# The first router's second pass goes on beside the end of its first pass, and its one-hots are multiplied on VectorE

## The chip, the cores and the metric

One core of a Trainium2 chip runs the whole program in one launch. The metric is the time of one execution in microseconds (us), on the device. Engines are named as in the profile: PE (TensorE: matrix products; PEld is its loading of weights), DVE (VectorE), ACT (ScalarE), POOL (GpSimd) and SP (the queue that issues most DMAs). Each engine works through its own instructions in order.

## The reference

The input x is 8 sequences of 512 tokens with 256 features, float32. Three sublayers follow one another, each on the layer-normalised x and added to x: half of a mixture-of-experts feed-forward, a sparse attention (each token attends to its 8 most similar earlier ones), and again half of the same feed-forward. The feed-forward is

```python
probs = softmax(xf @ gate_w.T); weights, idx = top_k(probs, 2)
weights = weights / weights.sum(-1)
out_all[e] = (silu(xf @ w1[e].T) * (xf @ w3[e].T)) @ w2[e].T      # 8 experts, 512 hidden
result = sum over the token's 2 experts of weight * out_all[expert]
```

Only the two chosen experts of each token need to be computed.

## The kernel before, in words

**Tiles.** The 4096 tokens make 8192 (token, expert) pairs in each feed-forward. A router sorts them by expert into tiles of 256 slots (`SLOTS`), in two halves of 128 rows. A tile does `fetch_weights` (one DMA of 1.5 MB from SP, its row read out of `wrow`), `fetch_rows` (two indirect gathers on POOL, L649, by the `tokens` table), `turn` (four transposes `ptx` on PE, L688, and their copy `xT` on DVE, L690), four times `up` (eight PE instructions `ph`, L699; `silu` on ACT, L707; the product `g` on DVE, L708), twice `down` (`py` on PE, L714) and twice `put` (scaling on ACT, L725, and an indirect DMA on POOL that adds the rows to `out`, L726). Weights and rows are fetched three tiles ahead.

**The first router's two passes.** `route` is a generator that goes on by one small step at each `next`. It runs twice for the first feed-forward: for sequences 0 to 3 (`select` is `begin`, kind "full") and 4 to 7 (`others`, kind "rest", `share=True`); both have `times=True`. The first pass gives the tables of the first four tiles (0 to 3 below), the second those of the following ones (rest 0, rest 1, ...). A pass counts the pairs, works out each pair's slot (`dest` L448 to L451; `at` and its reductions, L457 and L319; `slot`, `lane`, `group`, `cell`, `value`, L460 to L469), and then, in eight turns r = 0, 4, ..., 28 of four columns, builds one-hots: `in_lane` (L504) and `in_group` (L509) on DVE, and `put`, which is `in_group` times `value` (L518) and times `wts`. In the first pass both products run on POOL (L518, L526). In the second the first runs on POOL and the second as four activations on ACT (L524). PE multiplies `put` and `in_lane` into `pl` (L494, eight instructions a turn). Along with it goes `select.choose` (`free`, `pk` L572, `rank` to `owners` L575 to L603, `pw` L606, `wrow` L612). At the end come the addition to the table (L539), its transposes `pT` on PE (L621), their copy `tableT` (L624), the products `po` (L629), and `tokens` and `wslot` (L642, L645); the gathers wait for `tokens`.

**The order.** All of this part stands under a schedule written by hand: each engine's queue is in the order of the program. A list of steps runs both passes side by side (`half(0)`, `half(1)`) between statistics and normalisations. A loop (L1057 to L1060) then takes the first pass to its end. After it, what is left of the second pass is in `routing`, and `side`, called some six times a tile between the tile's PE work, takes it on by one step each time (`route_on`). `side` also takes on the normalisation of sequences 4 to 7 on ACT (`opening`, L979) and later the attention.

```python
        while halves[0].gi_frame is not None:
            if begin.wrow is not None and tiles[0].w is None:
                tiles[0].fetch_weights()
            half(0)
        derive_parameters()
    routing = [halves[1]]
```

`derive_parameters` (L146 to L157) issues three ACT functions (Sigmoid, Exp, Ln), each with a load of its function table, and some small DVE operations.

Of the kernel before, what the change touches and what calls it, by code (L numbers as in the profile page):

```python
# [28 lines left out]
def kernel(  # L29
# [14 lines left out]
    nc = tc.nc  # L44
# [91 lines left out]
    def load_parameters():  # L136
        for n in range(P // DH):
            nc.sync.dma_start(wkq_sb[:, :, n, :], (wqT if n % 2 else wkT).rearrange("(k p) h -> p k h", p=P))
        nc.sync.dma_start(gain_sb, gain.to_broadcast([P, D]))
        nc.sync.dma_start(bias_sb, bias.to_broadcast([P, D]))  # L140
        nc.sync.dma_start(mix_in, log_mix.to_broadcast([P, 1]))
        nc.sync.dma_start(scale_in, log_scale.to_broadcast([P, 1]))

    def derive_parameters():

        nc.scalar.activation(mix, mix_in, AF.Sigmoid)  # L146
        nc.vector.tensor_scalar(rest, mix, -1.0, 1.0, ALU.mult, ALU.add)
        nc.vector.tensor_scalar(mix_gain, gain_sb, mix, None, ALU.mult)

        sp_abs = const.tile([P, 1], F32, tag="sp_abs", name="sp_abs")  # L150
        nc.vector.scalar_tensor_tensor(sp_abs, scale_in, -1.0, scale_in, ALU.mult, ALU.min)
        sp_exp = const.tile([P, 1], F32, tag="sp_exp", name="sp_exp")
        nc.scalar.activation(sp_exp, sp_abs, AF.Exp)
        sp_log = const.tile([P, 1], F32, tag="sp_log", name="sp_log")
        nc.scalar.activation(sp_log, sp_exp, AF.Ln, bias=1.0)
        nc.vector.scalar_tensor_tensor(scale, scale_in, 0.0, sp_log, ALU.max, ALU.add)
        nc.vector.tensor_scalar(scale, scale, 0.01, None, ALU.add)  # L157
# [106 lines left out]
    def clear_rows():  # L264
        for t in (rows_d, out):
            nc.sync.dma_start(
                t[:PAD, :].rearrange("(h p) d -> p h d", p=P), zeros.unsqueeze(1).to_broadcast([P, PAD // P, D])
            )
# [24 lines left out]
    def route(ffn, s0, S, select, times=False, share=False):  # L293
# [195 lines left out]
        def chunks(t, r):  # L489
            return t.rearrange("p i j -> p (i j)")[:, r : r + R].unsqueeze(2)  # L490

        def multiply(r, in_lane, put):
            for q in range(R):
                nc.tensor.matmul(  # L494
                    pl, lhsT=in_lane[:, q, :], rhs=put[:, q, :, :ng], start=(r + q == 0), stop=(r + q == 2 * J - 1)
                )
# [3 lines left out]
        for r in range(0, 2 * J, R):  # L500
            if len(built) > 1:
                multiply(*built.pop(0))
            in_lane = small.tile([P, R, P], F32, tag="in_lane", name=f"in_lane_{name}_{r}", bufs=3)
            nc.vector.tensor_tensor(  # L504
                in_lane, lane_of.unsqueeze(1).to_broadcast([P, R, P]), chunks(lane, r).to_broadcast([P, R, P]),
                ALU.is_equal,
            )
            in_group = small.tile([P, R, NG], F32, tag="in_group", name=f"in_group_{name}_{r}", bufs=2)
            nc.vector.tensor_tensor(  # L509
                in_group[:, :, :ng], group_of[:, :ng].unsqueeze(1).to_broadcast([P, R, ng]),  # L510
                chunks(group, r).to_broadcast([P, R, ng]), ALU.is_equal,
            )
            if not times:
                yield
                if built:
                    multiply(*built.pop(0))
            put = small.tile([P, R, 2, NG], F32, tag="put", name=f"put_{name}_{r}", bufs=3)
            (nc.gpsimd if times else nc.vector).tensor_mul(  # L518
                put[:, :, 0, :ng], in_group[:, :, :ng], chunks(value, r).to_broadcast([P, R, ng])
            )  # L520
            if share:
                for q in range(R):
                    w = wts.rearrange("p i j -> p (i j)")[:, r + q : r + q + 1]
                    nc.scalar.activation(put[:, q, 1, :ng], in_group[:, q, :ng], AF.Copy, scale=w)  # L524
            else:
                (nc.gpsimd if times else nc.vector).tensor_mul(put[:, :, 1, :ng], in_group[:, :, :ng], chunks(wts, r).to_broadcast([P, R, ng]))  # L526
            built.append((r, in_lane, put))
            next(choice, None)
            yield
# [405 lines left out]
    def load(b):  # L935
        tag, bufs = ("xin", 4) if b < HALF_B else ("x1", 3) if b < B - 1 else ("own", 2)
        xb = work.tile([P, NC, D], F32, tag=tag, name=f"xin_{b}", bufs=bufs)
        nc.sync.dma_start(xb, x[b].rearrange("(c p) d -> p c d", p=P))
        xin.append(xb)
# [19 lines left out]
    def keep_rows(b):  # L959
        nc.sync.dma_start(seq_rows(out, first_ffn, b), xin[b])  # L960
# [24 lines left out]
    def gates(b):  # L985
        first_ffn.gates(b, columns[b])

    halves = [
        route(first_ffn, 0, HALF_B, begin, times=True),
        route(first_ffn, HALF_B, HALF_B, others, times=True, share=True),  # L990
    ]

    def half(i):
        next(halves[i], None)
# [43 lines left out]
    with tc.manual_schedule():  # L1038
        def load_columns(b):
            nc.sync.dma_start(columns[b].rearrange("p k t -> p (k t)"), xT[b].rearrange("p k t -> p (k t)"))  # L1040

        for b in range(HALF_B):
            load_columns(b)
            if b:
                load(b - 1)
        load(HALF_B - 1)
        clear_rows()
        for b in range(HALF_B, B):
            load_columns(b)
            load(b)  # L1050
        load_parameters()
        for step in steps:
            for f, b in step:
                f(b)
        for b in range(HALF_B):
            keep_rows(b)
        while halves[0].gi_frame is not None:  # L1057
            if begin.wrow is not None and tiles[0].w is None:
                tiles[0].fetch_weights()
            half(0)  # L1060
        derive_parameters()
    routing = [halves[1]]

# [19 lines left out]
    def finish_on():  # L1083

        nonlocal ended
        if finishing:
            b, steps = finishing[0]
            next(steps, None)
            if steps.gi_frame is None:
                finishing.pop(0)  # L1090
                ended = b + 1
                if ended in routes:
                    routing.append(route(*routes[ended]))
# [177 lines left out]
```

## Time and profile before

| what | value |
|---|---|
| median of 3 runs | 1052.44 us (1049.25 to 1053.2) |
| the profiled execution, its own time | 1052.27 us |
| its span, first to last instruction | 1050.5 us |
| mean granted TensorE clock | 0.985 |
| first `up` of tile 0 starts | 77.41 us |
| `up` of tiles 1, 2, 3, rest 0, rest 1 starts | 92.83, 115.81, 128.25, 141.24, 152.04 us |

The page gives the busy time of each engine, then groups of instructions by line with the idle time ahead of them; "PE pl_f L494 <- POOL put_f L518" is PE's wait at line 494 for what POOL wrote at line 518. In the timeline a row holds start, duration (from the first start to the last end of merged ones), engine, line, operation, output and inputs, and in brackets the engine's idle time ahead of it and what ended it. A table by stretch of time gives each engine's busy time in it, then the granted clock, the DMA engines' share and GB/s.

### The profile page before, as it was taken

Reading aid. Unit: us, or ns where it says so; the run is one execution under the profiler, and the core shown is the slowest. Engines: PE = TensorE matmul, PEld = TensorE weight load, DVE = VectorE, ACT = ScalarE, POOL = GpSimd, SP = SyncE. Lnnn points to the kernel's source line nnn. Section 1 sums busy time; section 2 is a strip of 40 time slices with the busy share of each in tenths; the row PEclk is TensorE's granted clock in tenths of the full one; section 3 lists DMA queues with packets and bytes.
Section 4 is the critical chain, followed back from the end, with each engine's and each line's share of the span. In section 5 each row is a group of like instructions: output and inputs, shape, how many; then the busy total and the mean of one; then the engine's idle time right before and its main releaser. Section 6 shows DMA issues by size and latency. Waiting matters only on the chain. (4 is left out here: it accounts for less than half of the span.)

```text
span 1050.5 us, 14816 instructions
## 1 busy us (share of the span) xinstructions
PE 985.9 (94%) x5008; PEld 853.0 (81%) x5008; DVE 545.5 (52%) x1838; ACT 383.7 (37%) x814; POOL 442.3 (42%) x434
## 2 busy tenths in 40 slices
PE   6768999999999999999999999999999999999984
PEld 6657888888787878878788787887888888889973
DVE  5954212124566665978649787587844422222221
ACT  1726222222645364363443633536313122212211
POOL 1133254546353354624425325253335454546343
PEclk9999999999999999999999999999999999999987
DMA  9557366666454546535436455363556565767665
GB/s 341 170 208 243 96 206 185 197 203 181 149 148 153 178 135 194 177 112 161 120 113 189 138 161 153 110 190 110 162 170 183 182 199 171 217 181 209 204 215 159
DMA packets 66164, 183.14 MB, mean 174 GB/s; under 512 B 8288, under 2 KB 51040, under 8 KB 56736
## 3 DMA queue, kind: packets, MB, share of 16 engines
q1 hardware_dynamic: 39216, 145.11, 39.9%
q0 software_dynamic: 26592, 36.98, 17.1%
q8 instruction: 44, 0.72, 0.3%
q14 instruction: 40, 0.33, 0.1%
q10 hardware_dynamic: 272, 0.01, 0.0%
HBM read 146.94 MB, written 35.13 MB: 173 GB/s over the span
## 5 line engine op out<-in xcount | busy, mean ns | idle before, releaser
L699 PE MATMUL ph_f_s<-xT_f_s,w_f_s 128*128 128x256 f32 (+1 forms) x2368 | 500.1, 365 | 4.2 <-ACTq L1218 3.4
L699 PEld LDWEIGHTS ph_f_s<-xT_f_s,w_f_s 128*128 128x128 f32 x2368 | 423.3, 193 | 71.4 <-issue 11.3
L726 POOL DMA_INDIRECT out<-y_f_s,tokens_f_s x133 | 215.8, 1622 | 399.5 <-ACT y_f_s L725 363.4
L708 DVE TENSOR_TENSOR g_f_s<-silu_f_s,ph_f_s 128x256 f32<-128x256 f32 (+1 forms) x296 | 117.1, 397 | 404.9 <-ACT silu_f_s L707 404.7
L714 PE MATMUL py_f_s<-w_f_s,g_f_s 128*128 128x256 f32 x1088 | 254.7, 384 | 0.0
L714 PEld LDWEIGHTS py_f_s<-w_f_s,g_f_s 128*128 128x128 f32 x1088 | 202.3, 192 | 25.3 <-issue 0.5
L707 ACT ACTIVATE silu_f_s<-ph_f_s 128x256 f32<-128x256 f32 (+1 forms) x296 | 108.4, 367 | 309.6 <-PE ph_f_s L699 303.4
L649 POOL DMA_INDIRECT xr_f_s<-rows_d,tokens_f_s x146 | 146.1, 1001 | 50.8 <-issue 32.3
L725 ACT ACTIVATE y_f_s<-py_f_s,wslot_f_s 128x256 f32<-128x256 f32 x133 | 56.3, 471 | 197.3 <-PE py_f_s L714 195.5
L707 ACT ACT_TABLE_LOAD x41 | 52.6, 1283 | 8.0 <-PE ph_f_s L699 7.4
L688 PE MATMUL ptx_f_s<-ident,xr_f_s 128*128 128x128 f32 x288 | 45.0, 277 | 10.4 <-DMA xr_f_s<-rows_d,tokens_f_s 10.4
L690 DVE COPY xT_f_s<-ptx_f_s 128x512 f32<-128x512 f32 x72 | 49.2, 683 | 9.4 <-PE ptx_f_s L688 9.4
L494 PE MATMUL pl_f<-put_f,in_lane_f 128*128 128x156 f32 (+4 forms) x256 | 43.9, 325 | 7.8 <-POOL put_f L518 4.0
L688 PEld LDWEIGHTS ptx_f_s<-ident,xr_f_s 128*128 128x128 f32 x288 | 36.0, 142 | 18.2 <-DMA xr_f_s<-rows_d,tokens_f_s 8.0
L494 PEld LDWEIGHTS pl_f<-put_f,in_lane_f 128*128 128x128 f32 x256 | 41.2, 230 | 10.2 <-POOL put_f L526 4.9
L750 POOL TENSOR_TENSOR own<-xn_at,mix_gain 128x1024 f32<-128x1024 f32 x8 | 19.5, 2434 | 59.7 <-DVE a_f L199 32.3
L1161 POOL MEMSET apart<- 128x1 f32 x62 | 44.0, 709 | 0.0
L825 ACT ACT_TABLE_LOAD x31 | 39.8, 1283 | 2.4 <-DVE nmax L814 1.9
L518 POOL TENSOR_TENSOR put_f<-in_group_f,value_f 128x184 f32<-128x184 f32 (+1 forms) x16 | 9.9, 621 | 72.1 <-DVE free_f_s L565 41.4
L783 PE MATMUL psim<-xnT_at 128*128 128x128 f32 (+3 forms) x128 | 40.0, 435 | 0.0
L844 PE MATMUL pm<-xn_at,exT 128*128 128x256 f32 x160 | 39.9, 380 | 0.0
L844 PEld LDWEIGHTS pm<-xn_at,exT 128*128 128x128 f32 x160 | 29.8, 190 | 3.7
(250 smaller groups left out, 901.0 us busy)
## 6 DMA issues: line engine op xcount, KB each, us to landing
w_f_s<-in_wexp SPq DMA_DIRECT2D x73, 1536.0 KB, 6.9
rows_d<-xn_f SPq DMA_DIRECT2D x16, 512.0 KB, 3.2
columns<-in_xT SPq DMA_DIRECT2D x8, 512.0 KB, 8.3
xin<-in_x SPq DMA_DIRECT2D x8, 512.0 KB, 9.2
out<-xin SPq DMA_DIRECT2D x8, 512.0 KB, 5.4
x<-out SPq DMA_DIRECT2D x8, 512.0 KB, 3.9
out<-x SPq DMA_DIRECT2D x8, 512.0 KB, 5.0
xr_f_s<-rows_d,tokens_f_s POOLq DMA_INDIRECT x146, 3.8
```

What stands on the lines that cost most here:

```text
L494: nc.tensor.matmul(pl, lhsT=in_lane[:, q, :], rhs=put[:, q, :, :ng], start=(r + q == 0), stop=(r + q == 2 * J - 1))
L649: nc.gpsimd.indirect_dma_start(out=dst, out_offset=None, in_=table, in_offset=bass.IndirectOffsetOnAxis(ap=index.bitcast(U32), axis=0),)
L688: nc.tensor.transpose(pt[:, k, h * P : (h + 1) * P], xr[:, k * P : (k + 1) * P], ident)
L690: nc.vector.tensor_copy(self.xT, pt)
L699: nc.tensor.matmul(ph[:, n, slots], lhsT=wn[:, k, f * P : (f + 1) * P], rhs=self.xT[:, k, slots], start=(k == 0), stop=(k == KD - 1),)
L707: nc.scalar.activation(s[:, slots], ph[:, 0, slots], AF.Silu)
L708: nc.vector.tensor_mul(self.g[:, f, slots], s[:, slots], ph[:, 1, slots])
L714: nc.tensor.matmul(self.py[:, h, :], lhsT=self.g[:, f, h * P : (h + 1) * P], rhs=self.w2[:, f, :], start=(f == 0), stop=(f == KF - 1),)
L725: nc.scalar.activation(y, self.py[:, h, :], AF.Copy, scale=self.routed.wslot[:, c])
L726: add = nc.gpsimd.indirect_dma_start(out=self.acc_d, out_offset=bass.IndirectOffsetOnAxis(ap=self.routed.tokens[:, c].bitcast(U32), axis=0 ...
L844: nc.tensor.matmul(pm[:, :D], lhsT=exTs[c][:, s * P : (s + 1) * P], rhs=after if c == 0 and s == 1 else xn[:, s, :], start=(s == 0), stop= ...
L1161: nc.gpsimd.memset(apart, 0.0)
```

## The change

The loop at the end of the opening takes the second pass on by one step with each step of the first, and in the second pass (`share`) DVE does the first product instead of POOL. The second product stays on ACT.

```diff
             put = small.tile([P, R, 2, NG], F32, tag="put", name=f"put_{name}_{r}", bufs=3)
-            (nc.gpsimd if times else nc.vector).tensor_mul(
+            (nc.gpsimd if times and not share else nc.vector).tensor_mul(
                 put[:, :, 0, :ng], in_group[:, :, :ng], chunks(value, r).to_broadcast([P, R, ng])
             )
...
             if begin.wrow is not None and tiles[0].w is None:
                 tiles[0].fetch_weights()
             half(0)
+            half(1)
         derive_parameters()
```

In each engine's queue this moves the following. DVE: `at`, `slot` to `value`, and the turns 0, 4 and 8 with their puts, `free`, `rank` to `owners` now stand ahead of the first pass's `tokens`; turn 12 stands ahead of tile 0's `xT`; turns 16 to 24 stand in tile 0, turn 28 behind tile 1's `xT`. PE: `pk`, `pl` of turns 0 and 4 and `pw` stand ahead of tile 0, the other six `pl` groups within tile 0, the second pass's `pT` and `po` in tile 1 (before: in tile 2). ACT: `put` of turns 0 to 12 ahead of the table loads of `derive_parameters`, the Ln load behind tile 0's first `silu`, and one more Silu load behind that. POOL: the eight products are gone, and rest 0's gathers stand ahead of tile 2's accumulates (before: behind them). SP: the order is the same.

## The prediction

> **What bounds the kernel now.** The page's busy shares come first, because they say whose time can be saved; then the waits of PE from 77 to 152 us, the stretch that the diff touches; then the timeline around the two waits, and the granted clock by stretch.
>
> ```profile
> PE 985.9 (94%) x5008; PEld 853.0 (81%) x5008; DVE 545.5 (52%) x1838; ACT 383.7 (37%) x814; POOL 442.3 (42%) x434
> ```
> PE is busy 94% of the span. From about 150 us on it hardly waits, so what moves its work there by some us moves the end as much. The gaps lie ahead of that.
>
> ```profile
> PE pl_f L494 <- POOL put_f L518: 4.0, 1, 4.0
> PE ptx_f_s L688 <- DMA xr_f_s<-rows_d,tokens_f_s: 1.8, 1, 1.8
> ```
> Between 77 and 152 us PE waits twice at length: once for a GpSimd one-hot product of the second pass, once for a gather. The timeline shows why:
>
> ```profile
> 71.10 0.17 DVE L642 TENSOR_TENSOR tokens_f_s<-po_f_s,cell_of 128x8 int32<-128x8 f32 x1 [1.96 <-PE po_f_s L629]
> 77.41 8.77 PE L699 MATMUL ph_f_s<-xT_f_s,w_f_s 128*128 128x256 f32 x32 [0.78 <-DVE xT_f_s L690]
> ...
> 99.45 1.38 POOL L649 DMA_INDIRECT xr_f_s<-rows_d,tokens_f_s  x1 [0.30 <-issue]
> 100.86 1.37 POOL L518 TENSOR_TENSOR put_f<-in_group_f,value_f 128x312 f32<-128x312 f32 x2
> 101.63 2.45 PE L494 MATMUL pl_f<-put_f,in_lane_f 128*128 128x156 f32 x8 [4.04 <-POOL put_f L518]
> ```
> VectorE had that put's one-hot by 93.2 us, but GpSimd's queue held two accumulates (94.29, 96.24) and two gathers (98.12, 99.45) ahead of it. The last column is the wait: 4.04 us of an idle PE. Then the clock:
>
> ```profile
> 86.00:92.80 6.80, 6.80 (x43) 6.08 (x41) 5.35 (x15) 5.22 (x17) 2.39 (x3) 1.00 0.78 263
> 92.80:101.60 8.80, 4.79 (x27) 4.03 (x25) 2.95 (x7) 6.56 (x19) 6.49 (x7) 0.97 1.03 323
> 101.60:106.00 4.40, 4.37 (x17) 4.10 (x18) 0.97 (x1) 1.11 (x4) 1.34 (x2) 0.66 0.93 311
> 141.20:152.00 10.80, 10.80 (x53) 9.51 (x53) 2.28 (x5) 2.38 (x6) 5.33 (x5) 1.00 0.66 195
> ```
> The column before the last two is the granted clock: 0.66 behind the gap. The last row is a tile undisturbed: 10.80 us, all of it PE.
>
> **Unit prices, from the timeline, start to start.** Four 256-column products of `up` (eight instructions): 1.73 us (silu at 82.76 and 84.49). One `pl` group of eight: 1.06 (88.84 to 89.90). VectorE: in_lane 0.60, in_group 0.40 (89.76, 90.36, 90.76). The new VectorE put, 312 elements, stands in the trace in the second router: 0.48 us, so a dependent in_group and put take 0.52 + 0.40, and a triple 1.52.
>
> **Price 1: the first tile starts later.** The listing of the changed build's order puts this on VectorE, in one queue, between `dest` (its last operation at 66.27) and the first tokens:
> - the two `at` products and reductions, 1.39 (81.79 to 83.18): the table add (L539) goes from 67.07 to 67.95;
> - slot to value 0.70 (83.52 to 84.24), triple 0 (1.52) and two `free` operations (0.15): tableT starts at 67.95 + 0.22 + 0.70 + 1.52 + 0.15 = 70.54, not 68.46; PE's transposes would be ready at 69.35, so VectorE sets it;
> - tableT 0.60, triples 4 and 8 (3.04), rank to owners (0.79): tokens at 74.97 instead of 71.10.
>
> That is **3.87 us later**. PE's own order is no later: `pk` ends at 71.7, `po` (1.87) at 73.6, two `pl` groups at the slow rate (2.24 each, from 101.63 to 103.87) at 78.1, `pw` at 78.7, and the first gathered rows land at 74.56 + 3.87 = 78.43, the second at 79.6. GpSimd has nothing ahead of the gathers, ACT's put parts (1.11 each) end before their `pl`. xT_0 waits behind triple 12 on VectorE, which ends at 77.7, before 80.54. So `up` starts at 77.41 + 3.87 = 81.28. Bounds: three puts at GpSimd's mean of 0.747 add 3 x 0.27 = 0.8; at VectorE's 152-element row, 0.31, they take off 0.5. I take the row of the same engine and size.
>
> **What is saved, from tile 0 to the second rest tile.** Before, `up` of tiles 0, 1, 2, 3, rest 0, rest 1 starts at 77.41, 92.83, 115.81, 128.25, 141.24, 152.04: 74.63 us. Its ledger: five tiles at 10.80 = 54.0; eight `pl` groups 8.48; `pk` and `pw` 0.61; `pT` and `po` 1.64 (12.44 - 10.80); first `up` group slow 1.72 (3.45 instead of 1.73); the wait 4.04; slow products behind it 1.5 (2.24 and 2.08, instead of 1.06 and 1.73); rest 0's late gather 2.19 (12.99 - 10.80). Sum 74.2; 0.4 is unassigned and stays.
>
> After:
> - The wait and its slow products go: **-5.54**. The puts no longer queue on GpSimd.
> - Two `pl` groups, `pk` and `pw` run in the gap ahead of tile 0, where PE waits for rows: **-2.73**.
> - Rest 0's gather goes from behind tile 2's accumulates to ahead of them, because the pass's tokens, at 124.80 before, come with tile 1's end at about 110: **-2.19**. Its other conditions are met: the last normalised rows are written at about 109 us, the gather issues at about 118, and its rows are wanted at about 131. SP's order is the same, and its weight fetches still wait for PE, tile by tile.
> - New: ACT in tile 0. Its queue now holds five table loads instead of four (1.28 us each); two of them fall inside tile 0. From silu_0 at 84.91: itself 0.40, Ln load and sp_log 1.52, two normalisations 0.98, put 16 1.04, Silu load 1.30, so silu_1 at 90.15; then two normalisations, a put that waits for its in_group and a silu in turn give silu_3 at 96.05 and g_3 at 96.87. PE, at 1.73 and 1.06 a group, wants g_3 at 95.92: **+1.0**. PE then reaches tile 1 at about 101.2. Bounds: 0 if ACT keeps pace; +1.4 more if put's four activations cost their busy mean (4 x 0.347 = 1.39, not 1.03).
> - The diff's VectorE work inside tiles 0 and 1 hides under ACT's waits (VectorE idles half of that stretch).
>
> Sum: -5.54 - 2.73 - 2.19 + 1.0 + 3.87 = **-5.6 us**. The profiled execution took 1052.27 (span 1050.5 and 1.77 around it, taken as constant); 1052.27 - 5.6 = **1046.7**. It lies 0.17 below the median of the runs shown, 1052.44, so no correction is made.
>
> **The clock of tile 0.** The first eight `up` products took 3.45 us at 77.41, the next 1.73: PE starts slow (the clock column reads 1.00 there, so the durations are the evidence). I keep that price, since 92-column `pl` groups stayed slow (2.02 for eight at 53.2, after 7 us of nearly unbroken work). But in the changed kernel 4.5 us of 156-column groups end at 78.1, and behind the gap at 101.63 just such a group and part of an `up` brought full speed after 2.8 us. [...]
>
> **Rivals.**
> - *PE is fast when tile 0 begins.* The 156-column groups release the clock, and the 3.2 us from 78.1 to 81.28, with transposes only, don't take it back. Then 1.72 goes: 1046.7 - 1.7 = 1045.0. For it: the speed-up at 104.4. Against: the 3.2 us, nearly the time after which the gap at 97.6 cost the clock. Chance 0.22.
> - *ACT becomes the bound of tile 0, or the gather stays late.* With ACT's longer activations (+1.4) and a GpSimd-priced put (+0.8) 1048.9; with rest 0's wait kept instead (+2.2) the same. For it: ACT's queue from 84.9 to 99.7 is full. Against: no such ACT pitch in the trace. Chance 0.22.
> - *Slower: tile 0 runs at half clock.* Its `up` groups come one at a time between `pl` groups that wait for ACT, so PE may never work densely enough. Tile 0 with its six groups is 17.2 us at full speed; each us of it at half clock costs one more. Beyond the 1.72 priced, 5.6 us of it pass the break-even; all of it gives 1046.7 + 15.4 = 1062. Against: the clock stayed 1.00 from 81 to 92.8 with the same alternation. Chance 0.04.
> - *That nothing moves* is excluded by the order listing.
>
> The forecast has 0.52. Half a per cent (5.3 us, to 1047.2) is about what a measurement of this kernel can tell from no change. The forecast lies beside that bound: some 0.31 of its 0.52 falls below, with 0.20 of the first rival and 0.02 of the second: faster 0.53. Nearly all else is same, 0.42, and the last rival with a little for what I haven't seen is slower, 0.05. The range takes in the first rival and most of the second: 1044.0 to 1049.5.
>
> **What would show it.** Tokens of the first pass at about 75 us and `up` at 81.3; no PE wait on a GpSimd put; first `up` group 3.45 us (or 1.7: first rival); g_3 and `pl` in tile 0 waiting for ACT about 1 us in all; tile 1 at 101, tile 2 at 113.6, rest 1 at 146.4; no wait for rows ahead of rest 0. It is wrong if tile 0 starts after 83, if tile 0 takes over 21 us, or if the lead at rest 1 is lost later.

## The result, and the profile after

The changed kernel takes 1045.07 us (median of 11 runs, 1040.95 to 1048.92), the kernel before beside it 1051.84 us (11 runs, 1049.25 to 1053.2). The ratio is 0.9937, with a 95% interval of 0.992 to 0.9955: faster by 0.6%, 6.8 us. The forecast was 1046.7, with 1044.0 to 1049.5 as its range.

The busy times hardly move (PE 985.9 us before, 984.2 after): what went is waits. The first fence is the page's line of busy times after the change, the second holds PE's waits between 77 and 152 us (in all, times, longest):

```profile
PE 984.2 (94%) x5008; PEld 852.3 (82%) x5008; DVE 547.5 (52%) x1846; ACT 384.9 (37%) x815; POOL 435.1 (42%) x426
```
```profile
PE ptx_f_s L688 <- DMA xr_f_s<-rows_d,tokens_f_s: 1.3, 2, 0.9
PE ph_f_s L699 <- issue: 0.8, 1, 0.8
PE py_f_s L714 <- DVE g_f_s L708: 0.7, 1, 0.7
```

The wait for a POOL product at L518, 4.0 us before, is gone from the second list. New in it is `py` waiting for `g`, 0.7 us. The timeline of PE shows where tile 0 now stands:

```profile
78.40 0.33 PE L688 MATMUL ptx_f_s<-ident,xr_f_s 128*128 128x128 f32 x1 [0.38 <-DMA xr_f_s<-rows_d,tokens_f_s]
79.66 0.55 PE L688 MATMUL ptx_f_s<-ident,xr_f_s 128*128 128x128 f32 x3 [0.93 <-DMA xr_f_s<-rows_d,tokens_f_s]
80.99 3.68 PE L699 MATMUL ph_f_s<-xT_f_s,w_f_s 128*128 128x256 f32 x8 [0.79 <-issue]
84.50 1.23 PE L494 MATMUL pl_f<-put_f,in_lane_f 128*128 128x156 f32 x8
85.56 1.89 PE L699 MATMUL ph_f_s<-xT_f_s,w_f_s 128*128 128x256 f32 x8
...
96.51 0.70 PE L714 MATMUL py_f_s<-w_f_s,g_f_s 128*128 128x256 f32 x2 [0.69 <-DVE g_f_s L708]
```

Read three things in it. Tile 0's first `up` is at 80.99 (77.41 before). It takes 3.5 us until `pl` starts at 84.50, the next one 1.73 (85.56 to 87.29): half speed, then full speed. The 0.69 in brackets at 96.51 is the wait for `g_3`. The table by stretches has PE's busy time behind the length of the stretch, and the granted clock in the column before the last two. The stretches here are those between the changes that this trace records of the clock:

```profile
74.22:77.63 3.41, 3.41 (x15) 1.00 0.09 25
77.63:81.04 3.41, 1.31 (x9) 1.00 0.30 93
81.04:84.45 3.41, 3.41 (x8) 0.50 0.38 115
```

The first change on record is at 77.63, and ahead of it the column reads 1.00 although the durations are those of half speed: the last `pl` products in the gap take 0.26 us each up to there, and 0.13 at full speed. So PE came to full speed at 77.63, fell to half at 81.04, just as tile 0 began, and was back at full speed at 84.45.

The starts of `up`, from the timelines, tell where each kernel of this study gains. From the first rest tile on all run at 10.80 us a tile, so the last column but one, 152.04 less the start of rest 1, is the lead that a kernel carries into the rest of its run. Each ratio is to runs of the kernel before beside it; the medians come from several sessions:

| kernel | tile 0 | tile 1 | rest 1 | lead at rest 1 | median, and ratio to before with its interval |
|---|---|---|---|---|---|
| before | 77.41 | 92.83 | 152.04 | 0 | |
| changed | 80.99 | 100.89 | 145.73 | 6.31 | 1045.07, 0.9937 (0.992 to 0.9955) |
| changed, second time | 81.12 | 101.14 | 145.98 | 6.06 | 1043.96, 0.9914 (0.9888 to 0.9939) |
| e1: product on DVE alone | 77.38 | 94.35 | 147.68 | 4.36 | 1045.27, 0.9951 (0.9935 to 0.9967) |
| e2: extra step alone | 80.97 | 100.99 | 145.82 | 6.22 | 1043.35, 0.993 (0.991 to 0.9949) |
| e6: 2.8 us more ahead of the tokens | 84.35 | 104.38 | 149.22 | 2.82 | 1048.12, 0.9971 (0.9954 to 0.9987) |
| e5: nothing ahead of the tokens | 77.51 | 102.17 | 147.01 | 5.03 | 1045.25, 0.9929 (0.9902 to 0.9955) |
| e3: added products (and loads moved) | 80.81 | 98.08 | 142.91 | 9.13 | 1038.96, 0.9886 (0.9865 to 0.9907) |
| e7: early loads | 80.93 | 99.85 | 144.69 | 7.35 | 1045.14, 0.9927 (0.9904 to 0.9949) |
| e8: early loads, added products | 80.96 | 98.23 | 143.06 | 8.98 | 1041.30, 0.9892 (0.9872 to 0.9911) |
| e9: as e8, tokens earlier | 79.62 | 96.89 | 141.72 | 10.32 | 1039.51, 0.9883 (0.986 to 0.9905) |
| e11: as e9 without added products | 80.25 | 97.52 | 142.35 | 9.69 | 1039.99, 0.9887 (0.9866 to 0.9907) |

Executions of one kernel differ by some 8 us, so a difference of 1 us between two of these medians says nothing; the starts in the traces do, each for one execution. They are what the conclusions below rest on, and the intervals are given where they settle something by themselves.

The leads hold in every trace to within 0.4 us up to 450 us. Behind that each execution gains or loses up to some 2 us at a time in places that the changes do not touch, so the profiled spans end 4.3 (changed, second time) to 14.2 us (e11) ahead of that of before, and not by their leads. The two executions of the changed kernel show it; the first two rows are the first time, the others the second:

```profile
751.58 3.70 PE L714 MATMUL py_f_s<-w_f_s,g_f_s 128*128 128x256 f32 x16
1010.32 3.84 PE L699 MATMUL ph_f_s<-xT_f_s,w_f_s 128*128 128x128 f32 x32 [0.61 <-ACTq L1219]
751.74 5.39 PE L714 MATMUL py_f_s<-w_f_s,g_f_s 128*128 128x256 f32 x16
1010.94 5.80 PE L699 MATMUL ph_f_s<-xT_f_s,w_f_s 128*128 128x128 f32 x32 [0.61 <-ACTq L1219]
```

The same products take 1.7 and 2.0 us longer in the second, with a granted clock of 0.50 on record for 3.41 us of the one stretch and 10.24 us around the other. Of its six runs, the two shortest (1039.48 and 1040.51) had a mean granted clock of 0.992 and 0.995, the two longest (1047.36 and 1047.93) 0.985 and 0.983.

### The profile page after: what moved, and what is told of

The parts are those of the page before. It is cut to its first block, busy times and chain, and to the rows that moved or that the text cites. A ratio compares the mean times of both kernels' runs of the same rounds, so it can differ in the third digit from the quotient of the medians.

```text
span 1043.8 us, 14809 instructions
## 1 busy us (share of the span) xinstructions
PE 984.2 (94%) x5008; PEld 852.3 (82%) x5008; DVE 547.5 (52%) x1846; ACT 384.9 (37%) x815; POOL 435.1 (42%) x426
## 5 line engine op out<-in xcount | busy, mean ns | idle before, releaser
L252 PEld LDWEIGHTS pg_f<-gwc,columns 128*128 128x128 f32 x128 | 27.5, 333 | 0.6 <-DVE gwc L124 0.6
```

## The experiments

### Each half of the change alone (e1, e2)

```diff
# e1, against the changed kernel: no extra step
             half(0)
-            half(1)
```
```diff
# e2, against the changed kernel: the product back on POOL
-            (nc.gpsimd if times and not share else nc.vector).tensor_mul(
+            (nc.gpsimd if times else nc.vector).tensor_mul(
```

> The kernel before with only the product moved from POOL to DVE in the second pass; the loop goes on with the first pass alone. Theory (the gain is the one wait for the product in POOL's queue): tile 0 starts at 77.4 us as before, PE's 4.04 us wait at tile 1 and the 1.5 us of half-clock products behind it go, rest 0's gather stays behind tile 2's accumulates with its 2.2 us. 1051.84 - 5.5 = 1046.3 us, a ratio to before near 0.995, so nearly the whole gain of the change with half of it. Rival (the step is what pays, because it takes the second pass out of tiles 0 to 2): no gain, 1050 to 1052 us.

> The kernel before with only the extra step of the second pass in the loop; its products stay on POOL. Theory: the products are issued to POOL before there are accumulates in its queue, so the 4.04 us wait goes as well, and DVE has three products of 0.52 us less ahead of the first pass's tokens: tokens at about 73.5 us (75.05 in the changed kernel), up of tile 0 at about 79.5, 1045.1 - 1.5 = 1043.6 us. The products taken over by DVE are then not needed for the gain. Rival (the move to DVE is needed: POOL's products slow DVE down or come late for PE): 1046 us or more, with PE waiting for a POOL product in tile 0.

**e1** came out as its theory had it: 1045.27 us, and tile 0 starts at 77.38 as before. Its PE timeline:

```profile
94.35 1.97 PE L699 MATMUL ph_f_s<-xT_f_s,w_f_s 128*128 128x256 f32 x8
96.16 1.22 PE L494 MATMUL pl_f<-put_f,in_lane_f 128*128 128x156 f32 x8
...
98.94 1.22 PE L494 MATMUL pl_f<-put_f,in_lane_f 128*128 128x156 f32 x8
...
111.59 3.62 PE L699 MATMUL ph_f_s<-xT_f_s,w_f_s 128*128 128x256 f32 x16
...
132.81 0.78 PE L688 MATMUL ptx_f_s<-ident,xr_f_s 128*128 128x128 f32 x4 [1.71 <-DMA xr_f_s<-rows_d,tokens_f_s]
```

From one `pl` to the next, 96.16 to 98.94, are 2.78 us, an `up` and a `pl` at full speed with no gap, where before there were 4.04 us of idle PE. Tile 1 takes 111.59 - 94.35 = 17.24 us instead of 115.81 - 92.83 = 22.98: this tile gains 5.74. The lead at rest 1 is only 4.36, because tile 0 took 16.97 us instead of 15.42: in this execution PE stayed at half speed for 5.5 us from its start (3.3 before), and a wait of 0.4 us for `free` came in. The 1.71 us in brackets at 132.81 are rest 0's gather, still late, since it still stands behind tile 2's accumulates in POOL's queue.

**e2** gains as much as the whole change (lead 6.22 against 6.31), so the product's move to DVE is not needed once the step is there. But its own theory fell in part: tokens came at 74.56, not 73.5, and tile 0 began no earlier. Three rows of POOL and one of DVE show why:

```profile
69.85 2.71 POOL L518 TENSOR_TENSOR put_f<-in_group_f,value_f 128x312 f32<-128x312 f32 x1 [5.08 <-DVE free_f_s L568]
72.52 0.70 POOL L518 TENSOR_TENSOR put_f<-in_group_f,value_f 128x312 f32<-128x312 f32 x1
73.70 0.71 POOL L518 TENSOR_TENSOR put_f<-in_group_f,value_f 128x312 f32<-128x312 f32 x1 [0.48 <-DVE rank_f_s L575]
```
```profile
72.59 0.97 DVE L509 TENSOR_TENSOR in_group_f<-group_of,group_f 128x312 f32<-128x312 f32 x1 [0.60 <-POOL put_f L518]
```

The first POOL product, beside a busy DVE, took 2.71 us, the two behind it 0.70 and 0.71. DVE waited 0.60 for the first, to get an `in_group` buffer back, and its next `in_group`, beside the second product, took 0.97 us instead of 0.48. Of the some 1.5 us that DVE no longer had to multiply it lost two thirds (1.09) to that, and tokens came 0.49 earlier. This rest went because the four transposes ran at half clock (0.47 and 0.90 us, against 0.33 and 0.55). Leads of 4.36 and 6.22 for the halves, and 6.31 for both, do not add because either of them removes the same 4.04 us wait.

### A later start of tile 0 (e6)

```diff
             tokens = const.tile([P, NH, take], I32, tag=f"tokens_{name}", name=f"tokens_{name}")
+            if self.kind == "full":
+                late = small.tile([P, 4, P], F32, tag="late", name=f"late_{name}", bufs=1)
+                for _ in range(4):
+                    nc.vector.tensor_tensor(
+                        late, lane_of.unsqueeze(1).to_broadcast([P, 4, P]),
+                        part_of.unsqueeze(1).to_broadcast([P, 4, P]), ALU.is_equal,
+                    )
```

> The changed kernel with four one-hot comparisons of 512 elements (0.60 us each, their result read by nobody) added on DVE right ahead of the first pass's tokens, so 2.4 us of delay. Theory (what lies on DVE ahead of the tokens moves the end one to one, as the 3.87 us of the forecast's price did): up of tile 0 2.4 us later, at 83.4, the lead at rest 1 smaller by the same, 1045.1 + 2.4 = 1047.5 us. Rival (a later start is taken up by waits further on, for ACT in tile 0, 0.7 us, and for rows): 1045.1 to 1046 us.

The four comparisons took 2.78 us, start to start (0.69 each and not 0.60), tokens came 2.68 later, `up` of tile 0 3.36 later, and the lead at rest 1 was 3.49 smaller; the median was 3.1 us above that of the changed kernel (4.2, if each is set against the runs of before beside it). So what stands on DVE ahead of the tokens moves the end at least one to one. What came on top is the clock; ACT's wait of 1.0 in tile 0 is gone here, since its Ln load came out earlier in this kernel's order, and the slower PE took back that gain. PE's rows, with the longer gap ahead of tile 0:

```profile
82.67 0.90 PE L695 MATMUL ptx_f_s<-ident,xr_f_s 128*128 128x128 f32 x3 [0.82 <-DMA xr_f_s<-rows_d,tokens_f_s]
84.35 3.78 PE L706 MATMUL ph_f_s<-xT_f_s,w_f_s 128*128 128x256 f32 x8 [0.78 <-DVE rest L147]
87.93 2.25 PE L494 MATMUL pl_f<-put_f,in_lane_f 128*128 128x156 f32 x8
90.01 1.89 PE L706 MATMUL ph_f_s<-xT_f_s,w_f_s 128*128 128x256 f32 x8
```

The transposes are at half clock (0.90 for three; 0.55 in the changed kernel), and so is the whole first `up` and most of the `pl` behind it (90.01 - 87.93 = 2.08 instead of 1.06).

### Nothing ahead of the tokens (e5)

```diff
             half(0)
-            half(1)
         derive_parameters()
+        for _ in range(6):
+            half(1)
```

> The loop goes on with the first pass alone, as before the change; behind it and the derived parameters the second pass takes six steps at once, with its products on DVE. So nothing of the second pass stands ahead of the tokens, and nothing of its PE work in the gap: the forecast's terms +3.87 and -2.73 are both undone. Theory: tokens at 71.1, up of tile 0 at 77.4 with a slow first group, rest 0's gather still ahead of tile 2's accumulates, tile 1 at about 99.5 (100.89 in the changed kernel), 1045.1 - 1.3 = 1043.8 us. Rival (PE waits for the pl groups' one-hots in tile 0, since DVE and ACT have only 4 us for them): 1045 us or more, with a wait of pl for ACT or DVE behind the first up.

The rival's time came (1045.25 us), but not by its wait. Tile 0 began at 77.51, tile 1 only at 102.17:

```profile
81.33 0.38 ACT L707 ACTIVATE silu_f_s<-ph_f_s 128x256 f32<-128x256 f32 x1 [6.56 <-PE ph_f_s L699]
81.61 3.10 ACT L524 ACTIVATE put_f<-in_group_f,wts_f 128x78 f32<-128x78 f32 x12
```
```profile
81.09 0.43 PE L572 MATMUL pk_f_s<-free_f_s,before 128*128 128x2 f32 x2
...
82.01 5.46 PE L494 MATMUL pl_f<-put_f,in_lane_f 128*128 128x156 f32 x22
...
87.80 0.38 PE L699 MATMUL ph_f_s<-xT_f_s,w_f_s 128*128 128x256 f32 x1
```

On ACT the first three puts (twelve activations) stand behind the first `silu`, for which ACT had waited 6.56 us, so PE got the first `pl` at 82.01 only. The wait itself is short, 0.2 us at most (the four `pk` products end at 81.93). What cost the time is that three `pl` groups took 5.79 us (82.01 to 87.80, `pw` included) instead of 3.3: by the durations PE stayed at half speed until 86.70, where the trace records its first change of the clock. That is 9.2 us at half speed, which cost 4.6, where the changed kernel paid 1.8. So the work moved from the gap into tile 0 cost more than its own length here. Whether that is because it no longer ran ahead of tile 0 is not shown (0.84 us of the slow stretch were `pk` products, to which the last section comes back): before the change nothing ran there either, and PE was slow for 3.3 us of tile 0 only (5.5 in e1).

### PE's clock, and ACT's table loads (e3, e7, e8)

```diff
# e3, against the changed kernel: products of zeros behind the first and the last transpose
                     nc.tensor.transpose(pt[:, k, h * P : (h + 1) * P], xr[:, k * P : (k + 1) * P], ident)
+                    if awake is not None and (k, h) in ((0, 0), (KD - 1, 1)):
+                        for _ in range(2):
+                            nc.tensor.matmul(awake, lhsT=self.rows[h][:, :P], rhs=zeros, start=True, stop=True)
...
```
```diff
# e7, against the changed kernel: the three functions ahead of the loop
-    def derive_parameters():
...
+    def open_parameters():
         nc.scalar.activation(mix, mix_in, AF.Sigmoid)
...
+    def derive_parameters():
+        nc.vector.tensor_scalar(rest, mix, -1.0, 1.0, ALU.mult, ALU.add)
+        nc.vector.tensor_scalar(mix_gain, gain_sb, mix, None, ALU.mult)
...
+        open_parameters()
         while halves[0].gi_frame is not None:
```

e8 has both edits.

> The changed kernel with four products of 128 by 256 zeros added on PE between the four transposes that stand ahead of tile 0's first up; their result is read by nobody. Theory of the clock (in the changed kernel it fell to 0.5 at 81 us, as tile 0 began, because PE had done 3.2 us of little but transposes): the added products keep it, the first up group takes about 1.75 us instead of 3.5, tile 1 starts 1.7 us earlier, 1045.1 - 1.6 = 1043.5 us. Rival (the first group is slow for another reason, or a few products do not hold the clock): 1045.1 us or up to 0.5 more, the granted clock still near 0.5 from 81 us.

> The changed kernel with ACT's Sigmoid, Exp and Ln (and their table loads) issued ahead of the loop, where ACT idles from 58.5 to 70 us; DVE's small operations on their results stay behind it. So no load but Silu's is left near tile 0 (in the kernel with added products, too, the Ln load had moved ahead of the first silu, so that run mixed two causes; this one takes one of them alone). Theory (the loads in tile 0 cost PE's wait for g_3 and no more): tile 0 starts at 81.0 with its slow first group of 3.5 us, tile 1 starts 0.7 to 1.0 us earlier than the 100.89 of the changed kernel, 1045.1 - 0.8 = 1044.3 us. Rival (the loads were the main cause of what the added products gained): 1041 us or less.

> The same early loads, and the four products of zeros added between tile 0's transposes (their result is read by nobody). Against the run with early loads alone it tells the clock's share by itself. Theory: first up group of 1.75 us instead of 3.5, tile 1 1.7 us earlier than in that run, 1042.6 us by the trace's stretch up to rest 1, near the 1039 of the first run with added products if that one's further 2 us belong to it. Rival (no effect of the clock): the same time as with early loads alone.

**e3** gained 2.8 us of lead where 1.7 was expected, and mixed two things. The first group was fast (80.81 to 82.64), but the edit, which touches PE's work alone, also moved ACT's Ln load: it came out ahead of the first `silu` (81.03) instead of behind it (85.11). So the queues are not in the order of the program to the letter, as the section on the kernel has it; what settles the order is not shown here. e7 and e8 take the two causes apart.

**e7**, the loads alone: tile 0 starts at 80.93 with its slow group (84.42 - 80.93 = 3.49), and `py` no longer waits for `g`:

```profile
PE ptx_f_s L689 <- DMA xr_f_s<-rows_d,tokens_f_s: 1.4, 2, 0.9
PE ph_f_s L700 <- issue: 0.8, 1, 0.8
```

Tile 0 takes 99.85 - 80.93 = 18.92 us instead of 19.90: the loads cost 0.98, as forecast (1.0). By its median alone, 1045.14, this kernel can't be told from the changed one.

**e8** against e7 is the clock by itself:

```profile
80.02 1.03 PE L692 MATMUL awake<-zeros,xr_f_s 128*128 128x256 f32 x4
80.96 1.99 PE L703 MATMUL ph_f_s<-xT_f_s,w_f_s 128*128 128x256 f32 x8
82.80 1.22 PE L495 MATMUL pl_f<-put_f,in_lane_f 128*128 128x156 f32 x8
```

The first `up` takes 1.84 us, and tile 1 starts at 98.23 instead of 99.85: 1.62 us from four products that nobody reads, in an idle gap. That they hold the clock does not hang on when it rises: in e3 it rose at 76.70 and was kept, in the changed kernel's second execution at 76.41 and was lost. e3 and e8 have the same lead (9.13 and 8.98) and nearly the same ratio to before, so the 2.3 us between their medians are not the edit.

### The tokens earlier (e9), and orders alone (e11)

```diff
# e9, against e8; e11 is the same without the products of zeros
+        turns = 0
         while halves[0].gi_frame is not None:
...
             half(0)
-            half(1)
+            if turns < 4:
+                half(1)
+            turns += 1
+        for _ in range(2):
+            half(1)
```

> Early loads and added products as in the run before it, and the second pass goes on in the first four turns of the loop only and twice behind it, so that its triple 8, rank to owners (2.3 us of DVE) stand behind the first pass's tokens instead of ahead of them, with all else in the same order. Theory (the forecast's price of 3.87 us for DVE's work ahead of the tokens is paid one to one and is avoidable in part): tokens at about 73.5 us instead of 75, up of tile 0 at 79.4, 1.4 us less than the run with early loads and added products. Rival (the rows, or PE's pl groups that end at 77.7, hold tile 0 where it was): no gain.

> Only changes of order, no added products: the changed kernel with ACT's loads ahead of the loop and the second pass in four turns of the loop and twice behind it. Theory (the terms add: 1.0 for the loads, 1.3 for the tokens, as the runs showed them one by one): tokens at 73.4, up of tile 0 at 79.5 to 79.7 with a slow first group again, unless the shorter stretch of transposes ahead of it (PE works until 77.4, then 2.1 us instead of 3.2) keeps the clock; rest 1 at 143.4 (145.73 in the changed kernel), 141.7 if the clock is kept. 1042.7 us, 1041 with the clock kept. Rival (only the added products gain, the orders do not add): 1044.5 us or more.

In **e9** tokens came at 73.30, 1.65 us before e8's; `up` started at 79.62, 1.34 before e8's, since the transposes now follow `pw` on PE without a gap. The lead at rest 1 is larger by the same 1.34: a start of tile 0 counts one to one again. In **e11**, orders alone, the first `up` ran at full speed without any added product:

```profile
78.06 0.48 PE L607 MATMUL pw_f_s<-visit_f_s,owners_f_s 128*128 128x35 f32 x2
78.34 1.12 PE L689 MATMUL ptx_f_s<-ident,xr_f_s 128*128 128x128 f32 x4
80.25 1.99 PE L700 MATMUL ph_f_s<-xT_f_s,w_f_s 128*128 128x256 f32 x8 [0.79 <-DVE xT_f_s L691]
82.08 1.22 PE L495 MATMUL pl_f<-put_f,in_lane_f 128*128 128x156 f32 x8
```
```profile
79.10:82.51 3.41, 2.62 (x15) 1.00 0.31 99
```

`pw` and the transposes follow one another until 79.46, and `up` starts 0.79 us later at full speed, 1.83 us for the group. But here PE was at half speed almost to the end of the transposes (0.48 us for `pw` and 1.12 for the four, against 0.31 and 0.60 at full speed): the clock rose at 79.10, and not at 77.63 as in the changed kernel. So in this execution it had not been kept across the gap, it came at its end. How much of the 1.7 us belongs to the order and how much to this moment is not shown by one trace. e11 takes 1039.99 us (5 runs, 1038.01 to 1041.83), a ratio of 0.9887 (0.9866 to 0.9907) to before. That is below the first interval of the changed kernel (from 0.992) and overlaps its second one, below (from 0.9888); the medians beside each other are 4.0 us apart, the leads 3.6. So this order, with no work added, is faster than before for certain, and by the traces faster than the change; of the 3.6 us some 1.7 are the first group's clock, for which there is one trace of e11.

### The changed kernel again (e12)

> The changed kernel itself, on the same chip and beside the same runs of before as the run with changes of order alone, so that the two can be set against each other. Theory: its ratio to before as at first, 0.992 to 0.9955, rest 1 at 145.7. Rival (its first ratio was of that chip and session): outside that interval.

The ratio, 0.9914 (0.9888 to 0.9939), overlaps the first one; its middle lies just below it, the median 8.5 us under before where the first was 6.8. The trace is of interest: the same program, tile 0 at 81.12, but here the slow stretch lasts longer. First the timeline of PE, then the clock's table:

```profile
81.12 3.78 PE L699 MATMUL ph_f_s<-xT_f_s,w_f_s 128*128 128x256 f32 x8 [0.78 <-DVE rest L147]
84.70 2.19 PE L494 MATMUL pl_f<-put_f,in_lane_f 128*128 128x156 f32 x8
86.72 1.89 PE L699 MATMUL ph_f_s<-xT_f_s,w_f_s 128*128 128x256 f32 x8
```
```profile
76.41:79.83 3.42, 1.50 (x11) 1.00 0.33 86
79.83:83.24 3.41, 2.63 (x8) 0.50 0.37 108
83.24:86.65 3.41, 3.41 (x12) 0.50 0.13 38
```

The clock rose and fell 1.2 us earlier than in the first execution (76.41 and 79.83 instead of 77.63 and 81.04), so the next 3.41 us held idle time and only the ones behind them were full of work. The slow stretch of tile 0 ran from 81.12 to 86.7, 5.6 us instead of 3.5, and yet tile 1 started only 0.25 us later (101.14): as PE was later, ACT was no longer late with `g_3`, and the wait of 0.7 us is not there. The prices of clock and loads are therefore not independent; whichever engine is later pays, and the other's delay hides.

## Why the prediction was right, step by step

- **The wait goes, -5.54**: right; measured by itself in e1, -5.74. It was the right reading of a wait on POOL: not the product held PE up, but the queue ahead of it; in e2 the products stayed on POOL, ahead of the accumulates, and the wait went too.
- **Rest 0's gather, -2.19**: right. In the changed kernel tile 3 to rest 0 is 134.93 - 124.13 = 10.80, with no wait; in e1, without the step, the wait stays (1.71).
- **`pl`, `pk` and `pw` into the gap, -2.73**: right as a sum. Tile 0 and tile 1 of the changed kernel are 19.90 = 10.80 + six `pl` at 1.06 (6.36) + the slow group (1.78) + 0.96, and 12.44 = 10.80 + 1.64, so nothing else is left in them.
- **Tile 0 later, +3.87**: 3.58. The chain on DVE was right to 0.1 us (tokens at 75.05, forecast 74.97; first rows at 78.40, forecast 78.43). The 0.3 is in the four transposes, which ran at full clock, 0.33 and 0.55 instead of 0.48 and 0.90. That each of these us counts, e6 and e9 showed.
- **ACT in tile 0, +1.0**: 0.96 in the trace, 0.98 by e7.
- **The slow first group, kept at 1.72**: 1.78, but half of the reason failed. I argued from the short gap and the 92-column groups that PE would be slow throughout. It did speed up in the gap, at 77.63, as the first rival had it, and lost the clock again as tile 0 began, at 81.04, behind a stretch in which PE had worked only 1.31 us of 3.41. That the size came out so close is luck: the same program paid 2.9 us for it in its second execution (20.02 for tile 0, without ACT's wait). The rival's price was right: e8 gained 1.62 where it said 1.72.
- **0.4 unassigned, kept**: it was not there after.

The sum of the lead is 5.6 + 0.3 (transposes) + 0.4 = 6.3, as measured at rest 1; the two spans differ by 6.7, with gains and losses behind rest 1 that the change does not touch. Of the other rivals, ACT did not become the bound (`put` took 1.11 a group, not 1.39), and tile 0 did not run at half clock throughout. Slow stretches of 5.6 us and 5.7 (e12, e6) and of 9.2 us (e5) did occur; at half speed they cost half their length, 2.8 and 4.6 us instead of 1.72, still well short of the 5.6 us more that this rival needed. The forecast lies 1.6 us above the median, and those terms explain 0.7 of it; the rest is within the spread of the runs.

What the forecast did not say is which half of the change pays. Both do, for the same wait, and the price of the step, 3.6 us, could be had for less: e11 pays 2.8 of it, and 1.0 less on ACT.

## What to carry to other kernels

When PE waits for a small product, look at the queue ahead of the product before moving it: here issuing it earlier (e2, a lead of 6.22 us) and moving it to another engine (e1, 4.36) each took the 4.04 us wait away, and the two together brought 6.31. Price what is put ahead of a table that all later work waits for one to one (in e6 tokens 2.68 us later cost 3.49 of the lead, in e9 a start 1.34 earlier gained 1.34), and keep there only what must be there. Work put into an idle gap ahead of a dense stretch can gain by itself, where PE then enters the stretch at full speed: 1.62 us in e8, from products that nobody reads. In the changed kernel a stretch of 3.41 us with 1.31 us of work, most of it transposes, stood behind that work, and the first `up` took 3.5 us instead of 1.73.

## What the runs showed of the hardware

- **The granted clock changed in steps of 3.41 us, and where the steps fell differed from one execution to the next.** In the trace of before, and in both of the changed kernel, the changes on record lie whole multiples of 3.41 us apart (before: 80.68, 101.16, 104.57). For the same program they stood at 77.63, 81.04 and 84.45 in one execution and at 76.41, 79.83 and 86.65 in another. Ahead of and in tile 0, the clock fell behind steps with 1.50 us of PE work or less (0.99 in e6, 1.29 in e7, 1.31 and 1.50 in the changed kernel), and stayed behind steps with 2.55 (e3), 2.62 (e11) and more (e8, e9). Back to full speed PE came there after a step with 3.26 us or more of work (3.26 in before, at 80.68; 3.41 in the changed kernel, at 77.63), not after 2.63 (e12) or 2.86 (e2); in before it came back at 104.57 after 2.94.
- **A step without idle time did not always keep the clock.** In the changed kernel's second execution the step from 748.84 to 752.25 was busy throughout, 2.1 us of it with products of 2 and 8 columns (`pk`, and `pg` at L252), and the clock fell. In the first execution a step ended, by the same spacing, at 750.05, in the midst of the same products, and the clock stayed. This is the 1.7 us at 751 between the two executions of one program. What made the clock fall there is not shown.
- **How long PE stayed slow varied.** After a gap, the first products ran at half speed for 3.5 us (changed kernel, e7), 5.6 (the same kernel again, 2.1 us more for one and the same program) and 5.7 (e6). In e5 it was 9.2 us: the step up to 83.29, one spacing ahead of its first change on record, held 3.33 us of work, 0.84 of it `pk` with two columns, and PE was still slow behind it. Why the `pl` groups of 92 columns in the opening stayed slow (2.02 us for eight at 55.36 in before, where eight of 156 columns take 1.06 at full speed) is open.
- **Ahead of the first change on record the granted clock read 1.00, also where PE was slow.** In e2 the first `up` takes 3.58 us (80.97 to 84.55) with a granted clock of 1.00 throughout, since the first change on record is at 85.16; in the changed kernel it takes 3.51 us with 0.50. The durations are the evidence.
- **Operations of POOL and DVE took longer beside each other in e2.** A POOL product of 312 elements took 0.71 us where DVE was idle (at 78.69) and 2.71 beside a busy DVE (at 69.85); beside another one, of 0.70, a DVE comparison of 312 elements took 0.97 us (at 72.59) instead of 0.48. Why is not shown.
